# Starting the second half of a row load from the GpSimd queue in a Toeplitz stage

## The chip, the cores and the metric

The kernel runs on one NeuronCore of a Trainium2 chip. The metric is the device time of one execution in microseconds. The core has a matrix engine (PE, with its weight loads shown apart as PEld), a vector engine (DVE), a scalar engine (ACT), GpSimd (POOL) and a sync engine (SP) that computes nothing and only begins DMA transfers. DMA transfers begun by SP and those begun by POOL run on the same 16 DMA engines, but stand in two different queues there: the profile calls SP's queue `q1 hardware_dynamic` and POOL's queue `q0 software_dynamic`.

## The reference

The input is a batch of 8 images of 56 x 56 tokens with 192 channels, in float32. Four residual layers follow one another, each after a group norm: `x = x + layer(group_norm(x))`. Layers 0 and 1 are gated Toeplitz layers, layer 2 is a depthwise 7 x 7 convolution with an MLP, and layer 3 is windowed attention. The change touches layers 0 and 1 alone, which compute:

```
p = silu(x @ p_w.T + p_b);  q = silu(x @ q_w.T + q_b);  v = silu(x @ v_w.T + v_b)   # 576 channels each
qv = q * v
o1 = toeplitz along the image rows (w) of qv, one 56-tap kernel pair per channel
o2 = toeplitz along the image columns (h) of qv, with another table
out = (p * (o1 + o2)) @ o_w.T + o_b
```

The Toeplitz tables come from a small MLP over the positions, times a decay. They depend on the weights only.

## The kernel before, in words

Four images are worked on at a time. Layer 0 and layer 1 are each cut into three kinds of work, written as Python generators that yield after each piece:

- `tno_qv` (L218) loads x, normalizes it, multiplies it with the q and v weights (PE, L257), adds the bias (DVE, L266), applies silu (ACT, L295), multiplies q by v (DVE, L298) and stores the product to the DRAM tensor `qv` with SP (L301). The product stands in a ring of three buffers named `t4`, so the fourth product has to wait until the first one's store has landed. The profile names these buffers `t`.
- `tno_toeplitz` (L359) reads `qv` back and applies the two Toeplitz products. It runs over `n` = 0 to 17: `blk = n // 2` is a block of 64 channels, `d = n % 2` the direction (0 along the rows, 1 along the columns). For each `n` it has a tile `q` (two buffers) and a tile of matrices `tm` (two buffers). `along` (256 matmuls a step, L394, with copies by ACT at L401) does the product; `turned` transposes the result (L411) and DVE puts it into `s` (L414 for d = 0) or adds it there (L417 for d = 1). `store` (L427) writes `s` to DRAM with POOL, four transfers for each half.
- `tno_out` (L463) loads the sums (L487, SP) and x (L114, SP), computes the gate p, multiplies, projects and stores the new x with POOL (L117).

The load of `q` differs by direction. For d = 1 it is one transfer of 3584 KB (L375). For d = 0 it is two transfers of 1568 KB, one for each `half` of the partitions (L372), and each moves 56 x 56 pieces of 512 bytes: one token's values of 32 channels in 4 images. After them comes the load of the matrices, 896 KB (L382). All of these are begun by SP. The loads for `n + 2` are begun once the eighth group of matmuls of step `n` is written out in program order, because the tile they fill is the one that step `n` has just read; the transfer therefore waits for those matmuls. The loads for n = 0 and n = 1 are begun ahead of the stretch.

`weave` (L633) mixes the three kinds of work by their estimated times into one order. There are four such stretches, one for each half of the images and each layer. In the profile they lie at about 480 to 1110 us, 1110 to 1970 us, 1970 to 2915 us and 2915 to 3600 us, and the text calls them stretch 0, 1, 2 and 3. Beside the Toeplitz work, stretch 0 holds a `tno_qv`, stretches 1 and 2 hold first a `tno_out` and then a `tno_qv` (from about 1586 and 2525 us), and stretch 3 holds a `tno_out`. The order of instructions on PE, ACT and DVE is the one written there. SP and POOL each run their own instructions in order: what one of them waits for holds up everything behind it in that queue.

Of the kernel before, what the change touches and what calls it, by code (L numbers as in the profile page):

```python
# [21 lines left out]
B, H, W, C = 8, 56, 56, 192  # L22
# [11 lines left out]
def view(ap, offset, dims):  # L34

    return bass.AP(ap.tensor, ap.offset + offset, [ap.ap[0], *dims])


class Net:
# [319 lines left out]
    def tno_toeplitz(self, j0, mats, qv, o):  # L359

        nc, p = self.nc, self.tz
        PR = H // 2

        def load(n):
            blk, d = divmod(n, 2)
            q = p.tile([128, H, 128], F32, name="q", bufs=2)
            if d == 0:
                for half in range(2):  # L370
                    of = qv[2 * blk + half, :T].rearrange("(h w) e -> w h e", w=W)
                    nc.sync.dma_start(q[64 * half : 64 * half + W], of)  # L372
            else:
                of = qv[2 * blk : 2 * blk + 2].rearrange("n (h w) e -> (n h) (w e)", w=W)
                nc.sync.dma_start(q.rearrange("p i e -> p (i e)"), of)  # L375
            return q

        def matrices(n):

            blk, d = divmod(n, 2)  # L380
            of = mats[d][2 * blk : 2 * blk + 2].rearrange("n p e -> (n p) e")
            nc.sync.dma_start(self.tms[n % 2][:, : 32 * H], of)  # L382

        def along(n, q, ot, g):


            tm = self.tms[n % 2]
            pt = self.bank2()
            for j in range(4):
                c = 4 * g + j  # L390
                for s in range(2):
                    for r in range(2):
                        rows = slice(64 * r, 64 * r + 56)
                        nc.tensor.matmul(  # L394
                            pt[64 * s : 64 * s + 64, r, j * 112 : (j + 1) * 112],
                            tm[rows, c * H : c * H + 64],
                            q[rows, PR * s : PR * s + PR, 4 * c : 4 * c + 4],
                            start=True,
                            stop=True,
                        )  # L400
            nc.scalar.copy(  # L401
                view(ot, 4 * g, [[112 * 32, 2], [32, 112], [1, 4]]),
                view(pt, 0, [[512, 2], [1, 112], [112, 4]]),
            )

        def turned(d, ot, s, r, i0, n):

            pz = self.bank2().rearrange("p k (i q) -> p (k i) q", q=128)
            for i in range(n):
                at = (r * PR + i0 + i) * 128  # L410
                nc.tensor.transpose(pz[:, i, :120], ot[:120, at : at + 128], self.ident[:120, :120])  # L411
            if d == 0:
                to = view(s, r * T + i0 * W + 55, [[W, n], [PR * W, 2], [-1, W]])
                nc.vector.tensor_copy(to, view(pz, 0, [[128, n], [64, 2], [1, 56]]))  # L414
            else:
                to = view(s, r * T + 55 * W + i0, [[-W, H], [PR, 2], [1, n]])
                nc.vector.tensor_add(to, to, view(pz, 0, [[1, 56], [64, 2], [128, n]]))  # L417

        def store(blk, s, half):
            for b in range(4):  # L420
                part, row = divmod(blk * DC + 32 * half, 128)
                if part < 4:
                    part += b // 2 * 4
                else:
                    part, row = 8, row + b // 2 * 64
                to = o[j0 + b % 2, part, row : row + 32, :]
                nc.gpsimd.dma_start(to, s[32 * b : 32 * b + 32, half, :])  # L427

        NS = 2 * (D1 // DC)
        loaded = []  # L430
        for n in range(2):
            loaded.append(load(n))
            matrices(n)
        yield 8.0

        late = []
        for n in range(NS):
            blk, d = divmod(n, 2)
            q = loaded.pop(0)
            ot = p.tile([128, 2 * PR * 128], F32, name="ot", bufs=1)  # L440
            if d == 0:
                s = p.tile([128, 2, T], F32, name="s", bufs=1)
            for g in range(8):
                along(n, q, ot, g)
                if g % 4 == 3:
                    if g == 7 and n + 2 < NS:
                        loaded.append(load(n + 2))
                        matrices(n + 2)
                    yield 3.2
                    for f in late:  # L450
                        store(*f)
                    late = []
            for u in range(8):
                turned(d, ot, s, u // 4, u % 4 * 7, 7)
                if u % 4 == 3:
                    yield 3.2
                    for f in late:
                        store(*f)
                    late = [(blk, s, u // 4)] if d == 1 else []
        for f in late:  # L460
            store(*f)
# [1179 lines left out]
```

## Time and profile before

| What | us |
|---|---|
| three runs of the kernel, lowest, median, highest | 6179.19, 6186.65, 6196.39 |
| the profiled execution's own time | 6175.88 |
| its span, first to last instruction | 6173.9 |
| PE busy in the span | 5692.9 |
| the four Toeplitz stretches together (480 to 3600 us) | 3120 |
| PE busy in them | 2898.2 |
| POOL busy in them | 200.5 |

The profiled execution is 0.17% shorter than the median of the three runs. A line of the timeline view has the start, the time taken, the engine, the line of the kernel, the operation, the tile written and the tile read, and the number of instructions merged; a bracket at its end is the idle time of the engine before it and what ended that. `SPq` is the SP queue: its time is that of beginning the transfer, not of the transfer. A line of the waits view has the waiting instruction, what released it, the total, the number of waits and the longest.

### The profile page before, as it was taken

The page shows a single profiled execution, that of the slowest core. Times are in us where ns is not written, and L with a number is a line of the kernel's source. Part 1 is how long each engine was busy: PE and PEld are TensorE (multiplying, and loading weights), DVE is VectorE, ACT ScalarE, POOL GpSimd, SP SyncE. Part 2 cuts the span into 40 slices and gives each one's busy share as a digit, 9 for nine tenths or more (in the row PEclk, how much of TensorE's full clock was granted, in tenths as well). Part 3 has the DMA queues.
Part 4 walks back from the last instruction along what each step waited for, and adds up shares of the span by engine and source line. Part 5 has one row for each costly group of instructions (what it writes and reads, how often), then busy time and mean ns, then how long its engine had stood idle before and what let it go on. Part 6 is the DMA issues. An engine that isn't in the chain of part 4 may idle for free.

```text
span 6173.9 us, 151657 instructions
## 1 busy us (share of the span) xinstructions
PE 5692.9 (92%) x68704; PEld 4463.1 (72%) x68704; DVE 2845.8 (46%) x4862; ACT 2154.4 (35%) x2738; POOL 639.2 (10%) x833
## 2 busy tenths in 40 slices
PE   5998989899999999999899989999999999988998
PEld 3777878788778788778778878885565444666666
DVE  6555555444555444556444443242222322555555
ACT  2334444223444323344333332224323433333332
POOL 0000000000000000000010010000000100333332
PEclk9999999999999999999999999999999999999998
DMA  7799997888676788776899856563444322444442
GB/s 261 168 225 250 268 239 213 230 230 238 187 205 183 194 240 245 183 208 180 218 250 252 260 171 235 211 218 123 158 166 133 96 63 61 72 87 96 89 91 58
DMA packets 1139557, 1119.74 MB, mean 181 GB/s; under 512 B 342529, under 2 KB 1076737, under 8 KB 1123489
## 3 DMA queue, kind: packets, MB, share of 16 engines
q1 hardware_dynamic: 1103328, 909.05, 54.6%
q0 software_dynamic: 35584, 200.98, 10.4%
q8 instruction: 540, 8.85, 0.6%
q14 instruction: 105, 0.85, 0.0%
HBM read 753.79 MB, written 389.15 MB: 185 GB/s over the span
## 4 chain that ended last, share of the span: by engine, by line
PE 74%; DVE 10%; DMA 7%; ACT 4%; issue 3%; POOL 2%; SPq 1%; DVEq 0%; POOLq 0%; ACTq 0%
PE bank L257 15%; PE bank L394 7%; PE bank L958 6%; PE bank L511 6%; PE bank L521 5%; PE bank L411 5%; PE bank L819 5%; PE bank L1038 4%; DMA qv<-t 3%; PE bank L526 3%; PE bank L543 3%; PE bank L1052 3%; PE bank L1179 1%; DVE t L266 1%; POOL e L1284 1%
## 5 line engine op out<-in xcount | busy, mean ns | idle before, releaser
L257 PE MATMUL bank<-wq,t 128*128 128x256 f32 (+4 forms) x7680 | 1278.0, 373 | 35.0 <-DVE t L266 12.5
L257 PEld LDWEIGHTS bank<-wq,t 128*128 128x128 f32 (+2 forms) x7680 | 1005.4, 190 | 278.5 <-issue 113.0
L295 ACT ACTIVATE t<-t 128x2048 f32<-128x2048 f32 (+2 forms) x288 | 427.7, 1489 | 758.1 <-DVE t L266 752.1
L401 ACT COPY ot<-bank 128x896 f32<-128x896 f32 x576 | 484.3, 921 | 410.3 <-PE bank L394 399.7
L266 DVE TENSOR_TENSOR t<-bank,wq 128x1024 f32<-128x1024 f32 (+3 forms) x480 | 517.9, 1111 | 207.7 <-PE bank L257 205.6
L394 PE MATMUL bank<-q,tm 56*64 56x112 f32 x18432 | 524.3, 266 | 78.4 <-issue 51.0
L394 PEld LDWEIGHTS bank<-q,tm 56*64 56x64 f32 x18432 | 483.8, 138 | 113.5 <-issue 82.8
L555 ACT ACTIVATE t<-bank,wo 128x448 f32<-128x448 f32 x448 | 247.6, 634 | 887.4 <-PE bank L526 863.4
L411 PE MATMUL bank<-ident,ot 120*128 120x120 f32 x4032 | 483.2, 279 | 73.2 <-ACT ot L401 39.3
L298 DVE TENSOR_TENSOR t<-t 128x1024 f32<-128x1024 f32 (+2 forms) x288 | 274.2, 955 | 588.2 <-ACT t L295 461.4
L411 PEld LDWEIGHTS bank<-ident,ot 120*128 120x128 f32 x4032 | 441.8, 147 | 122.1 <-ACT ot L401 44.9
L511 PE MATMUL bank<-t,wo 128*128 128x224 f32 x1792 | 387.8, 371 | 45.9 <-DVE t L493 43.8
L958 PE MATMUL bank<-z,w 128*128 128x448 f32 (+1 forms) x1344 | 413.6, 555 | 2.0 <-ACT h L967 2.0
L565 DVE SCALAR_TENSOR_TENSOR t<-bank,wo,t 128x448 f32<-128x448 f32 x112 | 76.4, 682 | 699.6 <-PE bank L550 698.9
L511 PEld LDWEIGHTS bank<-t,wo 128*128 128x128 f32 x1792 | 345.9, 199 | 63.6 <-issue 40.4
L521 PE MATMUL bank<-t,wo 128*128 128x224 f32 x1792 | 362.0, 355 | 12.0 <-issue 7.2
L582 DVE TENSOR_TENSOR t<-t,t 128x896 f32<-128x896 f32 x224 | 235.6, 1082 | 296.2 <-ACT t L555 296.2
L521 PEld LDWEIGHTS bank<-t,wo 128*128 128x128 f32 x1792 | 338.8, 191 | 20.1 <-issue 13.8
L819 PEld LDWEIGHTS bank<-xt,cm 113*112 113x112 f32 x3072 | 310.7, 178 | 36.6 <-issue 30.8
L958 PEld LDWEIGHTS bank<-z,w 128*128 128x128 f32 (+1 forms) x1344 | 182.4, 189 | 205.7 <-issue 197.4
L427 POOL DMA_DIRECT2D L_sum<-s x288 | 141.0, 496 | 1757.0 <-DVE s L417 1754.5
L819 PE MATMUL bank<-xt,cm 113*112 113x108 f32 (+2 forms) x3072 | 319.0, 264 | 4.0 <-ACT h L967 2.9
(147 smaller groups left out, 7075.1 us busy)
## 6 DMA issues: line engine op xcount, KB each, us to landing
q<-qv SPq DMA_DIRECT2D x36, 3584.0 KB
q<-qv SPq DMA_DIRECT2D x72, 1568.0 KB
L_sum<-s POOLq DMA_DIRECT2D x288, 392.0 KB, 7.5
t<-L_sum SPq DMA_DIRECT2D x112, 1008.0 KB
qv<-t SPq DMA_DIRECT2D x192, 512.0 KB
cm<-in_L_cm SPq DMA_DIRECT2D x96, 896.0 KB
tm<-L_mat SPq DMA_DIRECT2D x72, 896.0 KB
x<-t POOLq DMA_DIRECT2D x112, 336.0 KB, 5.4
```

Of the source, the lines that this page charges most:

```text
L257: nc.tensor.matmul(pp[:m, b, 256 * j : 256 * j + k], x[rows, j, 2 if part else b, s : s + m], w[rows, part, c0 + c : c0 + c + k],  start=p ...
L266: nc.vector.tensor_add(z[:m, c : c + k, :], view(pp[:m], 0, [[1, k], [256, 4]]), view(bias[:m], c0 + c, [[1, k], [0, 4]]),)
L295: nc.scalar.activation(z[:m, :n, :], z[:m, :n, :], AF.Silu)
L298: nc.vector.tensor_mul(prod[:m, :k], half[:, :, 0], half[:, :, 1])
L394: nc.tensor.matmul(pt[64 * s : 64 * s + 64, r, j * 112 : (j + 1) * 112], tm[rows, c * H : c * H + 64], q[rows, PR * s : PR * s + PR, 4 * c ...
L401: nc.scalar.copy(view(ot, 4 * g, [[112 * 32, 2], [32, 112], [1, 4]]), view(pt, 0, [[512, 2], [1, 112], [112, 4]]),)
L411: nc.tensor.transpose(pz[:, i, :120], ot[:120, at : at + 128], self.ident[:120, :120])
L511: mm(gs[c // 2][:, b, c % 2 * 256 : c % 2 * 256 + N], pw[:, 0, 128 * c : 128 * c + 128], xn[:, b], start=c % 2 == 0, stop=False,)
L521: mm(P[:, b, :N], ow[:, c, 0:128], g[:, 4 * b + c], start=c == 0, stop=False)
L555: nc.scalar.activation(pg[:, c], view(gs[i], c * 256, [[512, 2], [1, N]]), AF.Silu, bias=pb[:, 2 * i + c : 2 * i + c + 1],)
L819: nc.tensor.matmul(pc[:, 128 * e + 4 * m0 : 128 * e + 4 * m1], cm[:113, e, k, :], xt[:, m0 - 1 + k : m1 - 1 + k, c + e, :], start=n == 0 a ...
L958: nc.tensor.matmul(phs[c][:, s, :TT], w0[rows, part, at : at + 128], z[rows, Z[2 if part else s], :], start=part == flip, stop=part != flip,)
```

## The change

Of the two half loads of a d = 0 step, the second one (partitions 64 to 119) is begun by POOL instead of SP, except for n = 0. There are 9 such steps in a stretch (n = 0, 2, ... 16), so 8 half loads in each of the four stretches move, 32 in all, with 1568 KB each. The first half, the matrices and the d = 1 loads stay on SP, and no address, size or buffer changes.

```
         def load(n):
             blk, d = divmod(n, 2)
             q = p.tile([128, H, 128], F32, name="q", bufs=2)
             if d == 0:
-                for half in range(2):
+
+                for half, queue in enumerate((nc.sync, nc.gpsimd if n > 1 else nc.sync)):
                     of = qv[2 * blk + half, :T].rearrange("(h w) e -> w h e", w=W)
-                    nc.sync.dma_start(q[64 * half : 64 * half + W], of)
+                    queue.dma_start(q[64 * half : 64 * half + W], of)
             else:
```

More of the change, by code (lines that the diff above doesn't have):

```diff
@@ L369, in load @@
             if d == 0:
-                for half in range(2):
+                for half, queue in enumerate((nc.sync, nc.gpsimd if n > 1 else nc.sync)):
                     of = qv[2 * blk + half, :T].rearrange("(h w) e -> w h e", w=W)
-                    nc.sync.dma_start(q[64 * half : 64 * half + W], of)
+                    queue.dma_start(q[64 * half : 64 * half + W], of)
             else:
```

## The prediction

> **What bounds the kernel now.** I read the page first, then PE's waits in each stretch, then the timelines of SP, DVE and PE around one d = 0 load, then the issue and landing times of POOL's transfers.
>
> The page, engines and DMA queues (packets, MB, share of 16 engines):
>
> ```profile
> PE 5692.9 (92%) x68704; PEld 4463.1 (72%) x68704; DVE 2845.8 (46%) x4862; ACT 2154.4 (35%) x2738; POOL 639.2 (10%) x833
> q1 hardware_dynamic: 1103328, 909.05, 54.6%
> q0 software_dynamic: 35584, 200.98, 10.4%
> ```
>
> PE is the bound, so a change to transfers can win only what PE idles for a transfer: in the four stretches PE is busy 2898 of 3120 us, 222 us are idle. PE's waits in the tno_qv parts of stretch 1 (1560 to 1970 us) and stretch 2 (2500 to 2915 us), lines over 5 us:
>
> ```profile
> PE bank L411 <- DVE t L266: 10.6, 3, 4.6
> PE bank L394 <- DVE t L266: 7.0, 3, 3.4
> ...
> PE bank L411 <- DVE t L266: 12.0, 3, 5.7
> PE bank L394 <- DVE t L266: 6.9, 3, 3.7
> ```
>
> PE waits there for DVE's bias add (36.5 us in all). Why DVE is late shows the timeline of SP, then DVE, then PE, around the load for n = 14 in stretch 1:
>
> ```profile
> 1727.52 5.53 SPq L372 DMA_DIRECT2D q<-qv  x2
> 1733.10 9.94 SPq L382 DMA_DIRECT2D tm<-L_mat  x1
> 1743.14 4.64 SPq L301 DMA_DIRECT2D qv<-t  x2
> ...
> 1754.35 1.23 DVE L298 TENSOR_TENSOR t<-t 128x1024 f32<-128x1024 f32 x1 [7.77 <-DMA qv<-t]
> ...
> 1756.77 3.01 PE L411 MATMUL bank<-ident,ot 120*128 120x120 f32 x14 [4.56 <-DVE t L266]
> ```
>
> SP begins the first half in 0.34 us, then sticks 5.1 us on the second and 9.9 us on the matrices: its queue takes no more until earlier pieces have drained. The product store L301 waits behind that until 1743.14 and lands at 1754.3; DVE's next product needs that buffer, idles 7.77 us, and PE idles 4.56 us behind DVE. The same picture stands at each of the 32 d = 0 loads: over them SP's issue of the second half takes a median 7.5 us (253 us in sum), that of the matrices behind it 10.1 us (325 us). That 10.1 is so steady that I read it as the drain of one whole half.
>
> In stretches 0 and 3 PE idles differently, for nothing the profile names, inside the dense L394 matmuls (stretch 0, 480 to 1110 us; stretch 3, 3010 to 3600 us):
>
> ```profile
> PE bank L394 <- issue: 33.1, 12, 4.8
> ...
> PE bank L394 <- issue: 17.9, 13, 3.7
> ```
>
> The gaps that I looked at end 1.2 to 1.7 us after a 16 KB packet of the instruction queue is through (packet 576.2 to 577.2, gap to 578.4 us), so I read them as PE waiting for its next instructions while the DMA engines are full.
>
> **The change, part by part.** The sum is made against the profiled execution (6175.88 us, span 6173.9).
>
> (1) SP loses 32 issues. The matrices' issue takes the second half's place: it now waits only for the first half to drain (5 to 12 us, the old wait of the second half), not 10.1 us more. SP is free 10.1 us earlier at each load if the first half drains as before. But the second half now competes. By packet records, a 512-byte packet on SP's queue takes 39.8 ns on average, and POOL's queue merges pieces (x<-t, pieces of 896 bytes, shows packets of 4480 and 3584), with 174.7 ns for a 4096-byte one. So the moved half becomes about 392 packets x 174.7 = 68 engine-us instead of 3136 x 39.8 = 125: 4.3 us instead of 7.8 us on 16 engines. Where POOL's queue has work it takes 0.8 to 1.0 of the engines and SP's is left 0 to 0.2 (before the gap at 578.4: 0.82 against 0.18). So the first half is held up for 4 to 6 us, and the net is SP free 4 to 6 us earlier, and what follows no longer has the second half ahead of it in the queue.
>
> What that is worth: of the 36.5 us, 10.3 (4.61 and 5.72) come after d = 1 loads (the store at 1783.42 took 18.2 us behind 3584 KB), which stay; 2.8 (twice 1.42) end while DVE has no DMA to wait for. The six other places hold 2.28 + 1.32, 4.56, 3.41 in stretch 1 and 1.86 + 1.32, 4.90, 3.75 in stretch 2: 23.4 us. No single one is over 4.9, about what the store gains, so most should close; then ACT's silu and the bias adds come next on that chain. I take -21. Ends: -23.4, and 0 if the burst eats all that SP gains.
>
> (2) The stalls in L394. Those that lie in or just after the drain of a d = 0 load are 1.34, 1.78, 3.26, 3.85 us in stretch 0 and 0.82, 3.74, 3.19, 2.92, 2.90 in stretch 3, 23.8 us in all. Each load now keeps the engines busy 3.5 us less of a drain that lasts 24 to 33 us, which is an eighth or less, but the tail that meets the next `along` is what is cut: I take -5. Ends: -23.8 if all close; on the other side see rival B.
>
> (3) POOL gains 32 issues of 3136 pieces. The trace has no load on that queue. Nearest rows, POOL's issue time in ns (lowest, median, highest):
>
> ```profile
> L720 POOL DMA_DIRECT2D qv<-none x2: 1126/1223/1320, 2.0 to 3.3; - x2
> ...
> L117 POOL DMA_DIRECT2D x<-t x112: 744/773/869, 1132.4 to 4183.6; - x112
> ...
> L861 POOL DMA_DIRECT2D yd<-y x12: 552/571/576, 3776.5 to 4738.5; - x12
> DMA to landing us min/median/max: 8.2/9.5/11.0
> ```
>
> With 2016 pieces (L720) against 384 (L117) a further piece costs 0.28 ns, which gives 1.5 us; by the 0.78 ns a piece between L122 (128 pieces, 573 ns) and L117 it gives 2.9 us. I take 1.5, nearest in count. The first packets follow the issue by 1.3 to 5.7 us (L117) and 6.0 us (L720). The second half so lands 10 to 17 us after its issue; it is needed when `along` of n + 2 begins, 47 us later at the tightest I looked at (523.3 to 570.1). That slack hides it; nothing on PE.
>
> (4) POOL's new wait, for the matmuls of step n. Ahead of it in program order are the stores of `s` of the step before (L427, issued 3155.4 for a load at 3157.9) and one x<-t, both begun already by then. Behind it are x<-t stores that need later PE work: at 1260.5 the next is at 1273.1. They now stand behind the burst and land up to 8 us later; SP's L487 waits for them. Cover: SP already leaves 23.5 us between L487 at 1259.53 and 1283.01, and no DVE wait on that load is listed in these stretches. Cost 0; without that cover, 24 loads (stretches 1 to 3) x some us.
>
> (5) PE waits for two semaphores instead of one at the first matmul of 32 steps. A listed semaphore instruction takes 17 to 43 ns: at most 1.4 us, I take 0.
>
> (6) `s` stores in stretch 3: DVE waits 29.9 us in 3 waits for them, PE 1.15 + 3.13 + 5.36 behind that. The new half stands behind them in POOL's own queue, and SP's first half meets them as before. 0, within 9.6 either way.
>
> Sum: -21 - 5 = -26, thus 6150 for the profiled execution. The median of the runs is 10.8 higher, so 6186.65 - 26 = 6161.
>
> [...]
>
> **The rivals.** A measurement of this kernel can tell about 0.3%, 18.6 us.
>
> A, hidden: SP's freedom is eaten by the burst, since the same engines do the same work (term 1 at 0 to -8, term 2 at 0). For it: POOL's queue takes 0.8 to 1.0 of the engines. Against it: fewer engine-us, and stores no longer behind the second half. Time 6175 to 6187.
>
> B, slower: the burst starves PE of instructions. For it: 6 of the 11 stalls of over 1 us in stretch 0 (578.4, 645.7, 763.2, 834.3, 964.6, 1024.5; 3.2 to 4.8 us) lie in or at the end of a burst of `s` stores on POOL's queue. The new burst starts after L394 of step n and the next `along` begins 14 us later in stretch 0 (523.2 to 537.4), 19 us in stretch 3 (3035.7 to 3054.6). If it lasts beyond that, 16 loads of those stretches cost 3.5 us each, +56, less the 23: +33, time 6220. Against it: 2 to 6 us of start and 4.3 to 7.8 of data end before 14. It decides from a landing of 14 us on.
>
> C, larger gain: all of terms 1 and 2 close, -47: 6139.
>
> **How the numbers follow.** Forecast (mostly term 1) 0.5, C 0.08, A 0.25, B 0.17. Faster by over 0.3%: 0.5 + 0.08 less a few cases of the forecast that close to under 18.6 us, 0.54; within: A and those, 0.29; slower 0.17. The forecast's own range is 6148 to 6172. The one for all cases runs from C with 5 us of scatter (6134) to part of B (6205), since the granted clock differs by 0.95 to 0.98 between the stretches and 0.01 of 2898 busy us is 29.
>
> **What the changed profile would show.** L382's issue 5 to 12 us with no step of 10 behind an L372 of 5 to 12; L301 after a d = 0 load begun 4 us or more earlier; PE's waits on L266 in the tno_qv parts near 13 us instead of 36.5; POOL's L372 near 1.5 us; q0 up by 51 MB and about 12,500 packets. I am wrong if SP still sticks 15 us, if L394's issue stalls grow past 51 us, or if the POOL issue takes over 14 us.

## The result: 15 us less

Over ten runs of each kernel the changed one takes 6163.66 us (median, 6154.79 to 6174.21) and the one before 6178.82 (6162.04 to 6196.39; the 6186.65 that the prediction started from was the median of three). The ratio is 0.998, 95% interval 0.997 to 0.999. So the gain is real, but at 0.2% it is below the 0.3% that a measurement of this kernel was said to tell. A second comparison, told below, agrees: 0.9976 (0.9965 to 0.9988).

The page of the changed kernel, engines and DMA queues, and the new group of DMA issues (count, KB each, median us from issue to landing). Lines after 371 have moved down by one: L372 is now L373, L382 is L383, L394 is L395, L411 is L412.

```profile
span 6159.7 us, 151733 instructions
PE 5692.6 (92%) x68704; PEld 4462.1 (72%) x68704; DVE 2848.1 (46%) x4862; ACT 2155.2 (35%) x2738; POOL 689.3 (11%) x865
...
q1 hardware_dynamic: 1002528, 857.67, 49.9%
q0 software_dynamic: 50432, 252.42, 15.0%
...
q<-qv POOLq DMA_DIRECT2D x32, 1568.0 KB, 20.8
```

What to see: 51.4 MB have moved from q1 to q0, as forecast. But the shares show that this saved next to no engine time: q1 and q0 together took 54.6 + 10.4 = 65.0% before and take 49.9 + 15.0 = 64.9% now. By packet records a 4096-byte packet of the moved halves takes 357.1 ns on average (12,544 packets; the 174.7 ns of before came from 2,016 packets of the zero fill). A moved half so costs 392 x 357.1 ns = 140 engine-us, and SP's queue lost about 149 for each (the fall of its share, times 16 engines and the span, over 32 halves). The prediction had 68 against 125. Its 39.8 ns for a 512-byte packet on SP's queue was too low as well, as a mean over loads and product stores: between 3010 and 3600 us, where no product is stored, such a packet took 51.1 ns in the kernel before. With that, half a load is 3136 x 51.1 / 16 = 10.0 us, close to the 10.1 us that SP stuck; the 7.8 us of the prediction did not fit them.

PE's waits in the tno_qv parts of stretch 1 (1560 to 1970 us) and stretch 2 (2500 to 2915 us) of the changed kernel; columns are us in total, number of waits, longest:

```profile
PE bank L412 <- DVE t L266: 11.5, 3, 5.5
PE bank L395 <- DVE t L266: 3.2, 2, 1.8
...
PE bank L412 <- DVE t L266: 7.0, 3, 4.1
PE bank L395 <- DVE t L266: 2.8, 2, 2.0
```

These waits sum to 24.5 us, where the kernel before had 36.5 and the prediction expected about 13. In the second profiles, taken below, they are 21.9 and 30.0 us.

The timeline around the load for n = 14 in stretch 1, SP, then POOL, DVE and PE (start us, duration us, engine, line):

```profile
1720.99 0.34 SPq L373 DMA_DIRECT2D q<-qv  x1
1721.38 5.76 SPq L383 DMA_DIRECT2D tm<-L_mat  x1
1727.23 13.17 SPq L301 DMA_DIRECT2D qv<-t  x2
...
1722.18 1.56 POOL L373 DMA_DIRECT2D q<-qv  x1 [16.15 <-issue]
...
1747.86 1.23 DVE L298 TENSOR_TENSOR t<-t 128x1024 f32<-128x1024 f32 x1 [7.80 <-DMA qv<-t]
...
1750.27 2.06 PE L412 MATMUL bank<-ident,ot 120*128 120x120 f32 x9 [4.59 <-DVE t L266]
```

What to see: SP does come free as the change intends. The product store L301 is begun 6.2 us after the load's start, where it was 15.6 before. And yet DVE gets the store's buffer back 26.9 us after the load's start, where it was 26.8 before, and PE's wait is 4.59 us where it was 4.56. The store was begun 9.4 us earlier and came back no earlier.

Other places gained a little. DVE's row behind the load for n = 16 of the same stretch, in the kernel before (load begun at 1831.51) and in the changed one (1825.09):

```profile
1858.27 1.23 DVE L298 TENSOR_TENSOR t<-t 128x1024 f32<-128x1024 f32 x1 [6.04 <-DMA qv<-t]
...
1850.29 1.23 DVE L298 TENSOR_TENSOR t<-t 128x1024 f32<-128x1024 f32 x1 [4.47 <-DMA qv<-t]
```

That is 26.8 and 25.2 us after the load's start. Over the six places (n = 12, 14 and 16 of stretches 1 and 2) the buffer came back after 26.7 to 27.2 us before and after 24.2 to 26.9 us with the change, 1.5 us sooner on average, though SP was free 10 us sooner.

The stalls inside the dense L395 matmuls, stretch 0 (480 to 1110 us) and stretch 3 (3010 to 3600 us) of the changed kernel:

```profile
PE bank L395 <- issue: 30.2, 14, 3.8
...
PE bank L395 <- issue: 16.7, 13, 3.5
```

Together 46.9 us, 51.0 before. In the second profiles of each kernel it is 33.3 + 15.1 = 48.4 against 29.9 + 17.1 = 47.0. Nothing that two profiles can tell from scatter has gone.

Compared between the same PE instructions, the two tno_qv parts together are 824.9 us long before and 799.2 after; in the second profiles 810.1 and 795.7. Stretch 0 is 626.6 and 623.5, in the second profiles 622.9 and 623.2. So there is a gain where the prediction put its main term. What the rest of the kernel does can't be told from scatter: it is 11.5 us longer with the change in the first pair of profiles and 13.3 us shorter in the second (spans 6173.9 and 6159.7, 6174.0 and 6146.3 us). The question is what made the gain in the tno_qv parts.

### The profile page after: what moved, and what is told of

It is laid out like the page before. It is cut to its first block, busy times and chain, and to the rows that moved or that the text cites. A ratio compares the mean times of both kernels' runs of the same rounds, so it can differ in the third digit from the quotient of the medians.

```text
span 6159.7 us, 151733 instructions
## 1 busy us (share of the span) xinstructions
PE 5692.6 (92%) x68704; PEld 4462.1 (72%) x68704; DVE 2848.1 (46%) x4862; ACT 2155.2 (35%) x2738; POOL 689.3 (11%) x865
## 3 DMA queue, kind: packets, MB, share of 16 engines
q1 hardware_dynamic: 1002528, 857.67, 49.9%
## 5 line engine op out<-in xcount | busy, mean ns | idle before, releaser
L395 PE MATMUL bank<-q,tm 56*64 56x112 f32 x18432 | 516.9, 264 | 67.4 <-issue 46.9
L395 PEld LDWEIGHTS bank<-q,tm 56*64 56x64 f32 x18432 | 475.9, 137 | 104.2 <-issue 80.8
L412 PE MATMUL bank<-ident,ot 120*128 120x120 f32 x4032 | 481.2, 279 | 69.7 <-ACT ot L402 38.2
L412 PEld LDWEIGHTS bank<-ident,ot 120*128 120x128 f32 x4032 | 440.4, 147 | 118.2 <-ACT ot L402 43.7
L522 PE MATMUL bank<-t,wo 128*128 128x224 f32 x1792 | 366.0, 358 | 14.8 <-issue 6.4
L522 PEld LDWEIGHTS bank<-t,wo 128*128 128x128 f32 x1792 | 342.4, 193 | 23.4 <-issue 12.8
L415 DVE COPY s<-bank 128x784 f32<-128x784 f32 x288 | 259.3, 964 | 83.9 <-DMA L_sum<-s 43.4
## 6 DMA issues: line engine op xcount, KB each, us to landing
q<-qv POOLq DMA_DIRECT2D x32, 1568.0 KB, 20.8
```

Source lines behind the costliest of these rows:

```text
L395: nc.tensor.matmul(pt[64 * s : 64 * s + 64, r, j * 112 : (j + 1) * 112], tm[rows, c * H : c * H + 64], q[rows, PR * s : PR * s + PR, 4 * c ...
L522: mm(P[:, b, :N], ow[:, c, 0:128], g[:, 4 * b + c], start=c == 0, stop=False)
```

## The experiments

Three readings were to be told apart. *Freedom*: the gain comes from SP being free earlier at each d = 0 load (the prediction's term 1; theory 1 in the expectations). *Elsewhere*: it comes from other places or from the granted clock (theory 2). *Place*: what matters is how soon the bulk ahead of the store has drained, and for a moved half that depends on how many moved halves went before it (theory 3, formed after the first runs). Expectations were written before the runs they belong to, so each tells the theories as they stood then.

In all runs below the whole computation is done.

### The two kernels once more, and the change in two parts

Two runs repeat the kernels as they are.

> The kernel before once more, for a second profile: how far idle time and granted clock scatter by stretch with nothing changed. Ratio 1.000 within 0.1%. Theory 1 expects PE's waits for the bias add in the tno_qv parts at 33 to 40 us again; theory 2 expects the granted clock of 2500 to 2915 us to be up to 0.97 here as well, and that stretch 7 us shorter for it.

> The changed kernel once more, for a second profile. Theory 1 (SP is free earlier behind the d = 0 loads of the tno_qv parts, so the product stores start earlier) expects the ratio again at 0.997 to 0.999, PE's waits for the bias add in the two tno_qv parts at about 24 us against 36.5, and idle PE time there 10 to 16 us under the kernel before. Theory 2 (the gain of the profiled pair is mostly the granted clock, 0.97 against 0.95 there) expects that another profile shows the busy time as before and a gain of under 8 us.

Two split the change by place: `late_only` moves the second half only in stretches 1 and 2 from n = 10 on, which is where the product stores wait (8 of the 32 loads); `early_only` moves the other 24.

```
late_only:
-                for half in range(2):
+                for half, queue in enumerate((nc.sync, nc.gpsimd if stretch in (1, 2) and n >= 10 else nc.sync)):
-                    nc.sync.dma_start(...)
+                    queue.dma_start(...)
early_only: the same with
+    nc.gpsimd if n > 1 and not (stretch in (1, 2) and n >= 10) else nc.sync
```

> POOL begins the second half only for n = 10 to 16 of stretches 1 and 2 (8 of the 32 loads), the loads beside tno_qv. Theory 1 expects nearly the whole gain, 10 to 15 us of 6179 (ratio about 0.998). Theory 2 (the gain is not in those parts, but from the drain in stretches 0 and 3 and the clock) expects 0 to 4 us.

> POOL begins the other 24 second halves, those of stretches 0 and 3 and of n = 2 to 8 in stretches 1 and 2; the 8 of late_only stay on SP. Theory 1 expects 0 to 5 us of gain (the stalls inside the L394 matmuls of stretch 0 fell by 4.6 us in the profile). Theory 2 expects 10 to 15 us.

Measured, ratio to the kernel before with its 95% interval:

| run | ratio | us |
|---|---|---|
| before once more | 1.0006 (0.9995 to 1.0016) | 6175.08 |
| after once more | 0.9976 (0.9965 to 0.9988) | 6161.15 |
| late_only | 0.9994 (0.9982 to 1.0005) | 6169.87 |
| early_only | 0.9998 (0.9989 to 1.0007) | 6173.56 |

Neither part alone gains anything that the measurement can tell. By their middles the two parts do not add up to the whole, though by the low ends of their intervals they could (0.9982 and 0.9989), so the waits have to decide. That `early_only` gains nothing tells against *elsewhere*, which expected 10 to 15 us of it, and was to be expected by *freedom*. That `late_only` gains nothing was not, for SP does come free there. SP in `late_only` around the load for n = 16 of stretch 1, then DVE:

```profile
1821.35 0.34 SPq L373 DMA_DIRECT2D q<-qv  x1
1821.74 5.66 SPq L383 DMA_DIRECT2D tm<-L_mat  x1
1827.49 24.28 SPq L301 DMA_DIRECT2D qv<-t  x4
...
1850.16 1.22 DVE L298 TENSOR_TENSOR t<-t 128x1024 f32<-128x1024 f32 x1 [8.08 <-DMA qv<-t]
```

The store is begun 6.1 us after the load's start, and DVE has its buffer 28.8 us after it; at the same n it was 26.8 us in the kernel before. PE's waits in the tno_qv part of stretch 1 of `late_only`:

```profile
PE bank L412 <- DVE t L266: 9.6, 3, 6.7
PE bank L395 <- DVE t L266: 8.6, 3, 5.5
```

18.2 us, no less than the 17.6 of the kernel before (15.2 in its second profile). In its stretch 2, where SP comes free as early, they are 13.0 us, against 19.0 and 14.8. *Freedom*, taken alone, falls here.

### What the store waits for

If it is not the issue, it is the landing. The store stands behind the loads in SP's queue: the first half and the matrices. Two runs change that. `stores_pool` is the kernel before, with the product store begun by GpSimd's queue, so that no bulk load stands ahead of it; the loads stay as they were. `mats_on_pool` is the kernel before with the matrices of the even steps begun by GpSimd instead of the second half.

```
stores_pool:
-                lambda: nc.sync.dma_start(
+                lambda: nc.gpsimd.dma_start(
mats_on_pool:
-            nc.sync.dma_start(self.tms[n % 2][:, : 32 * H], of)
+            (nc.gpsimd if n % 2 == 0 and n > 1 else nc.sync).dma_start(self.tms[n % 2][:, : 32 * H], of)
```

> The loads as in the kernel before; the product stores (qv<-t) are begun by POOL instead of SP, so that no load stands ahead of them in their queue. If PE's waits for the bias add come from the stores' place behind the loads in SP's queue, they fall from 30 to 37 us to under 12 and the ratio is 0.995 to 0.997. If they come from the DMA engines being full (any queue would land them as late), they stay over 25 us and the ratio is 0.999 to 1.001. Slower than 1.003 would be a new wait: the x<-t and s stores behind product stores on POOL.

> Both halves on SP as before; the matrices behind them (896 KB, 128 pieces of 7168 bytes) are begun by POOL for even n over 1. Theory 1 expects SP's 10 us step not to go away but to pass to the next transfer behind the second half (a product store or L487 taking about 10 us), so no gain: ratio 0.9995 to 1.0005. If the matrices' own transfer were what holds SP, SP would be free 10 us earlier and the ratio 0.998.

`stores_pool`: 0.9867 (0.9848 to 0.9886), 6096.27 us against 6171.44, five times the gain of the change. PE's waits in the tno_qv parts of stretch 1 and stretch 2:

```profile
PE bank L411 <- DVE t L266: 2.8, 2, 1.4
...
PE bank L411 <- DVE t L266: 2.9, 2, 1.4
```

What is left are four waits of 1.4 us: at the two places where DVE waited for no DMA before, and at the two behind d = 1 loads. All six waits behind d = 0 loads are gone. The ratio is better than either expectation, and not all of it comes from these waits: between the same PE instructions the two tno_qv parts take 767 us (825 and 810 in the two profiles of before), the part ahead of 480 us 466 (480 and 477), and stretch 0 is 19 and 15 us shorter; products are stored there too. The issue and landing of the stores on POOL's queue:

```profile
L301 POOL DMA_DIRECT2D qv<-t x300: 611/887/953, 100.9 to 2906.3; - x150
DMA to landing us min/median/max: 2.3/5.7/15.0
```

A store lands a median 5.7 us after its issue. In the kernel before, the store at n = 14 began at 1743.14 and DVE had its buffer at 1754.35, 11.2 us later; in the changed kernel it took 20.6 us (1727.23 to 1747.86), having been begun earlier into a fuller queue.

`mats_on_pool`: 1.0001 (0.9989 to 1.0013). SP's timeline around a d = 0 load:

```profile
1732.90 8.73 SPq L372 DMA_DIRECT2D q<-qv  x2
1741.72 12.75 SPq L301 DMA_DIRECT2D qv<-t  x2
```

The 12.75 us spans two stores, which took 4.64 us at the same n in the kernel before, while GpSimd begins the matrices in 0.57 us: the step is back on SP, where with the matrices gone the product store stands in their place. In these two kernels it belongs to the transfer that comes next after two halves, not to the matrices. The six waits sum to 22.0 us, 23.4 before.

### The drain, and a second hardware queue

The prediction had taken it that POOL's queue shortens the drain. `on_act` starts the same 32 halves from ScalarE, whose queue is of the same kind as SP's (the profile calls both `hardware_dynamic`).

```
-                for half in range(2):
+                for half, queue in enumerate((nc.sync, nc.scalar if n > 1 else nc.sync)):
```

> The moved half is begun by ACT's queue instead of POOL's: also off SP, but pieces of 512 bytes on a hardware queue, not packets of 4096. Theory 1 (what counts is that SP is free 10 us earlier) expects the gain of the change or more, ratio 0.996 to 0.998, if ACT's issue stays near 0.35 us. Theory 3 (what counts is on which engines and in which packets the pieces drain) expects the PE waits of the tno_qv parts not under 30 us and a ratio of 0.999 to 1.001. If ACT sticks on the issue as SP does, 32 x 5 us on ACT show as PE waits for its copies and the ratio is over 1.003.

`on_act`: 0.991 (0.9891 to 0.9929), 6116.28 us. The page's DMA queues, then the issue of the halves on ACT (count, issue ns lowest/median/highest):

```profile
q1 hardware_dynamic: 1002528, 857.67, 48.5%
q0 software_dynamic: 35584, 200.98, 10.5%
q10 hardware_dynamic: 100800, 51.38, 3.7%
```

```profile
L373 ACTq DMA_DIRECT2D q<-qv x32: 313/313/588, 527.6 to 3416.2; - x32
```

And PE's waits in the two tno_qv parts:

```profile
PE bank L412 <- DVE t L266: 3.9, 4, 1.4
...
PE bank L412 <- DVE t L266: 4.8, 4, 1.7
```

From the load's start to the last packet of its matrices, median over the 32 loads: 26.5 us before, 26.3 with the change, 19.85 in `on_act`. The change starts the halves from elsewhere and drains them no faster; a second hardware queue drains them 6.6 us faster, and the six waits fall to 3.0 us. Neither expectation had this: by theory 1 the ratio was to be 0.996 to 0.998, by theory 3 about 1. The queues' shares say by what: q10 takes 3.7% of 16 engines x 6100.5 us for 100,800 packets, 36 ns each, where the same bytes cost POOL's queue 4.6% more (10.4 to 15.0).

### Does the drain depend on the place in the sequence

In the table, each for the loads n = 12, 14, 16 of a stretch: the mean time from the load's start until SP is free, the mean time until the matrices' last packet, and the sum of the three PE waits behind them (us).

| kernel, stretch | SP free | matrices through | PE waits |
|---|---|---|---|
| before, 1 | 15.9 | 24.9 | 11.57 |
| before, 2 | 16.5 | 25.0 | 11.83 |
| late_only, 1 | 6.2 | 26.2 | 15.32 |
| late_only, 2 | 6.4 | 24.5 | 10.15 |
| late_plus4, 1 | 5.9 | 23.3 | 8.02 |
| late_plus4, 2 | 6.5 | 26.3 | 15.68 |
| after, 1 | 6.0 | 23.7 | 7.75 |
| after, 2 | 5.6 | 23.1 | 6.95 |

The waits follow the third column and not the second: 10 us of freedom of SP move them nowhere, 1 us of drain moves three waits by some 2.7 us ((15.68 - 6.95) / (26.3 - 23.1) = 2.7). After `late_only` the low and the high stretches suggested the number of moved halves that went before: from n = 12 on, 1 to 3 in its stretch 1 and 5 to 7 in its stretch 2; in the changed kernel, which has 8 in each stretch, 13 to 15 and 21 to 23, that is again 5 to 7 beyond a multiple of 8. `late_plus4` tests it: `late_only` with four more moved halves in stretch 0, which makes it 5 to 7 in stretch 1 and 9 to 11 in stretch 2. If the count decides, stretch 1 should come out as in the changed kernel and stretch 2 as stretch 1 of `late_only`; by *freedom* both should stay as in `late_only`, since the same loads move.

```
+    nc.gpsimd if stretch < 3 and n >= 10 else nc.sync
```

> late_only, and in stretch 0 also n = 10 to 16 on POOL: 4 moved loads stand ahead of those of stretch 1, where late_only has none and the changed kernel 12; the 8 late loads themselves are as in late_only and in the changed kernel. [...]

The flip came: PE's waits in the tno_qv parts of stretch 1 and stretch 2 of `late_plus4`:

```profile
PE bank L412 <- DVE t L266: 8.0, 3, 4.9
PE bank L395 <- DVE t L266: 3.1, 2, 1.9
...
PE bank L412 <- DVE t L266: 9.6, 3, 6.8
PE bank L395 <- DVE t L266: 8.9, 3, 5.8
```

Stretch 1, where the loads are the same as in `late_only`, fell from 18.2 to 11.1 us; stretch 2 rose from 13.0 to 18.5. The time is 0.9996 (0.9983 to 1.0008), so what one stretch gains the other loses. This also tells why the two halves of the change did not add up: with all 32 moved, both late stretches fall on the good count.

`early_only`, run before this theory, holds a check of it at the same n. Its loads n = 6 and 8 have counts 10 and 11 in stretch 1, but 14 and 15 in stretch 2, where the changed kernel has 18 and 19. The matrices are through after 28.4 and 28.9 us in its stretch 1, as with the change (28.1 and 28.2), and after 24.1 and 25.7 us in its stretch 2, where the change has 29.1 and 27.9 (second profile 28.7 and 28.8). So 2 and 3 beyond a multiple of 8 are slow and 6 and 7 are quick for the same n. For n = 2 and 4 no such order is shown.

What carries such a count no run shows. `start6` and `start12` were meant to change it by small transfers between the moved halves: the changed kernel with a transfer of 2 partitions of 4 bytes on POOL's queue after each moved half, and one of 6 or 12 partitions ahead. That such transfers would change it was the author's estimate.

```
+                if n > 1:
+                    self.shift(2)      # gpsimd DMA of 2 partitions x 4 bytes into a tile that nothing reads
...
+                self.shift(6)          # start12: 12
```

> The changed kernel with 33 extra transfers of 4-byte pieces on POOL: one of 6 partitions before the first stretch, then one of 2 partitions after each moved half. [...]

> [...] Theory 1 expects the same ratio as start6 within 0.1%.

They came out alike: 0.9969 (0.9953 to 0.9986) and 0.9971 (0.9959 to 0.9984), the six waits 7.98 + 7.48 and 7.68 + 8.39 us against 7.75 + 6.95 with the change alone. But the edit did not do what it was meant to do. The issue times of the small transfers in `start6`:

```profile
L361 POOL DMA_DIRECT2D spare<-in_pmat x33: 499/499/520, 6.4 to 64.4; - x33
```

There all 33 ran ahead of the first stretch (6.4 to 64.4 us), so none stood between two moved halves; `start12` differs in the size of the one ahead alone, and its waits came out alike. So what is shown is that the drain goes with the count of moved halves before, as long as POOL's queue carries nothing else that is new; what carries that is open. And the count is not all: in `after_and_stores` below, with the changed kernel's counts but the product stores in the same queue, the matrices of the late loads are through after 26.4 and 26.6 us instead of 23.7 and 23.1.

### Both levers together

If the landing of the store is what counts, moving it off SP should leave nothing for the change to gain. `after_and_stores` is the changed kernel with the store edit, `act_and_stores` is `on_act` with it.

> The changed kernel with the product stores on POOL too. If the change worked by the stores' place in SP's queue, it has nothing left to give here: ratio as stores_pool alone, 0.985 to 0.989. If the moved halves now stand ahead of the product stores in POOL's queue, the stores land later and the ratio is 0.990 to 0.997.

> on_act and stores_pool together. If they close the same waits in the tno_qv parts and on_act shortens stretch 0 besides (its stalls fell from 37 to 21 us), the ratio is 0.983 to 0.986; if they added up fully it would be 0.978. Over 0.989 would mean that the two get in each other's way.

`after_and_stores`: 0.9938 (0.9926 to 0.9951), 6137.24 us; that is worse than the store edit alone (0.9867). Now store and half share POOL's queue. PE's waits in stretch 0 of `after_and_stores`; those for the bias add sum to 20.8 us over all lines, where they are 2.0 us with the change alone and 5.4 with the store edit alone:

```profile
PE bank L395 <- DVE t L266: 16.4, 4, 5.0
PE bank L395 <- issue: 10.1, 6, 3.3
```

The longest landing of a store there is 24.9 us, 15.0 in `stores_pool`. Beside these stores the change costs time, as it puts a bulk load ahead of them.

`act_and_stores`: 0.9845 (0.9829 to 0.9862), 6076.93 us, the fastest of all, 1.55% below the kernel before.

The stalls in L395 of stretch 0 are down to 12.8 us there and to 16.6 in `on_act`, from 33.1 and 29.9 in the two profiles of before. So what the prediction's second term wanted to cut does yield when the load drains faster. It can yield otherwise too: `after_and_stores` has 10.1 us of these stalls with a drain as long as before (27.1 us), beside its 20.8 us of waits for the bias add.

## Why the prediction was right in time and wrong in its main step

Predicted were 26 us less; measured are 15. The time lies in the range, on the side of the forecast, but the likeliest outcome (faster by over 0.3%) did not come: the gain falls between the forecast and rival A, and half of A's mechanism is what happened.

- **Term 1, SP's freedom: the size of the freedom held.** SP was to come free 4 to 6 us earlier. Over the 32 loads its time from the load's start to being free went from 605.6 to 423.6 us, 5.7 us each. The mean hides two kinds: within 10 us at 16 loads, 17 to 25 us at the others, among them all of stretch 3.
- **Term 1, what it is worth: this is the step that failed.** The prediction held that no single wait is over 4.9 us, "about what the store gains, so most should close", and took -21. The same six waits measured 23.4 us before and 14.7 after (24.3 and 16.2 in the second profiles), -8.4 on average instead of -21. The store was begun some 9 us earlier, but its buffer came back 1.5 us earlier on average, and it comes back on landing. The waits closed by 1.3 us a place in stretch 1 and 1.6 in stretch 2, about what the drain gained there (24.9 to 23.7 us and 25.0 to 23.1 us), and that went with the place in the sequence.
- **Term 1, the price of the moved half.** 68 engine-us, by the 174.7 ns of the zero fill's packets; measured 140, at 357.1 ns. That row was of packets of the same size in another kind of transfer, a fill of DRAM that gathers nothing from 512-byte pieces. With the measured price (140 on POOL's queue against some 149 on SP's) the burst takes nearly all that the shorter queue gives, and the reason for the -21 is gone: this is rival A's argument.
- **Part of the 36.5 us was the chance of one profile.** The second has 30.0. The 10.3 us behind d = 1 loads are 2.85 in the second profile of the same kernel, and near that in all other profiles but the changed kernel's first (6.9). It was rightly left out of the sum, but "13 us left" was read off a number that does not repeat.
- **Term 2, the stalls in L394: -5 forecast, about -1 measured** (51.0 and 47.0 before, 46.9 and 48.4 after), within scatter. From the load's start to its matrices' last packet it takes as long as before (26.3 us against 26.5), so the eighth of a drain that it was to save was not there. Rival B's +56 did not come either: they did not grow past 51 us.
- **Term 3, POOL's issue: right.** 1.57 us (1548 to 1596 ns) against 1.5. The landing is later than thought, 20.8 us instead of 10 to 17, and past the 14 us from which rival B was to decide; it stayed hidden within the 47 us of slack, and no more stalls for PE's instructions came with it. So that point decided nothing.
- **Terms 4 and 5 at nothing: nothing seen against them.** They were not tested by a run of their own; `early_only`, which holds 24 of the 32 new waits, is at 0.9998.
- **Term 6: right.** PE's waits of over 1 us behind the `s` stores in stretch 3 are 9.6 and 11.3 us in the two profiles of before, 10.7 and 12.4 after.

What makes up the 15, then: in the two tno_qv parts the profiles show 8.4 us less of the six waits, and 9 us less of the time outside PE's gaps, in which the same matmuls ran faster (772 to 763 us, means of two profiles; the last section). No term of the sum had the second. With about 1 us of stalls that is 18 us, where the runs show 15; two profiles of the kernel before differ by 7 us in the time outside the gaps alone, so the split is rough. A missing term of the right sign covered part of the miss in term 1. The time itself was also helped by chance: the median of ten runs of the kernel before is 7.8 us under that of three, from which the prediction counted, so 6163.66 lies 3 us from the 6161 forecast while the gain is off by 11.

## What to carry to other kernels

When an engine waits for a buffer that a store has to give back, ask when the store lands, not when the issuing engine comes free: being begun earlier into a queue full of loads gave nothing here (0.9994), and giving the small store a queue without bulk ahead of it gave 1.3%. Price a transfer from packets of its own shape and direction on that queue; here a neighbour's packets were off by a factor of 2.0. And profile the kernel before twice before pricing waits of a few us, for 7 of the 36.5 us that this prediction started from did not come back.

## What the hardware showed that was not expected

**The same matmuls took less time where the gaps between them closed (768.8 to 752.6 us).** The view by windows, second profile of the kernel before, tno_qv parts of stretches 1 and 2 (length, then busy us of PE, PEld, DVE, ACT, POOL, then granted clock, DMA share, GB/s):

```profile
1560.00:1970.00 410.00, 390.20 (x4377) 331.01 (x4376) 230.78 (x249) 182.70 (x200) 18.18 (x37) 0.97 0.69 193
2500.00:2915.00 415.00, 395.06 (x4385) 334.76 (x4386) 233.37 (x246) 181.78 (x199) 19.49 (x41) 0.96 0.70 197
```

and about the same parts in `stores_pool`:

```profile
1556.00:1941.00 385.00, 380.48 (x4271) 322.60 (x4264) 232.71 (x241) 180.92 (x197) 72.04 (x101) 1.00 0.72 207
2457.00:2841.00 384.00, 376.74 (x4326) 320.64 (x4327) 228.36 (x245) 179.59 (x198) 69.41 (x96) 0.99 0.72 208
```

The granted clock is 0.96 to 0.97 in the one and 0.99 to 1.00 in the other. The windows do not hold quite the same instructions; counted between the same 8,842 matmuls, PE's gaps over 0.3 us shrink from 41.6 to 15.0 us, and the time outside them, in which the same work is done, from 768.8 to 752.6 us. The changed kernel lies between (36 and 33 us of gaps, 763 us outside them). So each us of gap closed came with some 0.6 us of faster matmuls ((768.8 - 752.6) / (41.6 - 15.0)). In the first profile of the kernel before it is 49.4 us of gaps and 776 us outside them. The single gaps are under 7 us. The two go together over the profiles taken; that the gaps set the clock was not tested by itself.

**SP's queue held back its issuer; ACT's, which carried the 32 halves alone, did not.** A half of 3136 pieces is begun in 0.31 us on ACT's queue (0.59 us at most; 100,800 packets on it, 3150 for each of the halves) and in 0.34 us as the first on SP's, but the next transfer on SP takes longer to begin, a median 7.5 us for the second half and 10.1 for the matrices in the kernel before; with the matrices moved away the step went to the transfer behind them (`mats_on_pool`), so it is read as waiting for the pieces ahead to drain. The packet records fit that: at n = 14 of stretch 1 in the kernel before, 1562 of the 6272 pieces were through when the second half's issue ended and 4650 when the matrices' did, 3088 more, where a half has 3136. GpSimd's queue takes the same half in 1.57 us and sends its packets from about 5 to 21 us after the load's start.
